# Gated cross attention: scores of two slots made in a row, and three results that share one PSUM bank

## The chip, the cores and the metric

The kernel runs on one core of a Trainium2 chip. Its time is the device time of one execution in microseconds (us), and the median of three executions is given. A core has a matrix engine (TensorE, PE in the profile, with its weight loads as a row of their own, PEld), a vector engine (VectorE, DVE), a scalar engine for activations (ScalarE, ACT), GpSimd (POOL) and SyncE (SP), which issues nearly all DMAs of this kernel. PE writes its results to PSUM, which has eight banks of 2 KB in each of 128 partitions; a bank holds 512 float32 columns. DVE and ACT read them from there.

## What is computed

Two layers of a gated block run over 8 sequences of 512 tokens with 256 features. The change lies in the first part, a cross attention with 16 heads of 64 features, whose weights are multiplied by a gate made from boxes:

```python
emb = box_relational_embedding(boxes)            # sines and cosines of log distances
g = relu(einsum('bnmd,hd->bhnm', emb, Wg) + bg)
q, k, v = projections of layernorm(x), ctx, ctx
a = einsum('bhqd,bhkd->bhqk', q, k) / sqrt(64)
mn = softmax(log(clip(g, 1e-6, None)) + a)       # = max(g, 1e-6) * exp(a), normalised
out = einsum('bhqk,bhkd->bqhd', mn, v) @ Wo.T + bo
x = x + tanh(g_xattn[0]) * out
```

After it come an attention with a mixture of experts, a second attention and a spiking feed-forward layer. The change leaves those alone.

## The kernel before

The cross attention is done in 32 steps `i`, one for each block of 128 queries. A step has 8 slots `p`, one for each pair of heads. Queries, keys and values have been projected ahead of the steps and lie in DRAM. The order of the instructions on PE, ACT and DVE is that of the program text (`tc.manual_schedule(engines=MANUAL)`, lines 547 to 595): each of these engines takes its instructions strictly in the order in which the loop writes them. The queue of SyncE is ordered by the compiler's planner. Buffers come from pools: a tile with a tag and `bufs=n` has n places, and a new tile of that tag waits until the last reader of the tile n before it is done. The pool `wk` (line 396) has two places unless a tile says otherwise, and the PSUM pool `ps` (line 397) has one.

What a slot p of step i does, in this order:

- `scores(i, p + 1)` (446): two matmuls over 64 rows each, one head each, into the two banks of `pS`; PE shows each as two records, so there are four. Then DVE takes the row maxima `nm` (459) and ACT makes the exponentials `e` (462) of both heads.
- `half()` (555), two or three times in a slot (`HALVES`): `gate_half` (422) makes a half block of the gates of the next step, two matmuls (four PE records) into one of two banks `pg`, and copies it to SBUF (441), on DVE in slots 0, 2 and 7 and on ACT in the others.
- `weigh(i, p)` (465), after the first half: eight transposes of `e` into the two banks of `pT`, then one DVE instruction of 1024 elements (473), which multiplies them by the gates into `at`.
- `values(i, p - 1)` (478), after the second half: eight matmuls (sixteen PE records) of the last slot's `at` with the values, into `po`. After an odd pair DVE takes the reciprocal `rec` of the sums (497) and makes the outputs `o` of four heads (499).
- `outputs` (504), at the end of slots 1, 3, 5, 7: two transposes of `o` into `pt`, and one ACT copy to `oT` (514).
- `mix` (516), at the end of slot 2: eight matmuls (sixteen records) of the last step's `oT` with `Wo` into `pw`, then on DVE the bias (526) and the residual sum (528), and a DMA to DRAM.
- `features`: pieces of the gate features of later steps. On DVE: `turns` (325) at the end of slot 0, `whole` and `rest` (328, 332) at the end of slot 1, `rest_sizes` (81) in slot 2 after the scores, `offsets` (310) at the end of slot 4 (three instructions) and slot 5 (two), `clip` (319) at the end of slot 6. On ACT: `sines` (338, 339) in slot 2, `sizes` (316) at the end of slot 5, `log` (322) in slot 7. Sines and logarithm need other activation tables than the exponentials, so a table load stands ahead of each and ahead of the next exponentials.

PSUM is full: `pS` 2 banks, `pT` 2, `po` 1, `pt` and `pw` 1 (tag "m"), `pg` 2.

Of the kernel before, what the change touches and what calls it, by code (L numbers as in the profile page):

```python
# [11 lines left out]
F32 = mybir.dt.float32  # L12
I32 = mybir.dt.int32
AF = mybir.ActivationFunctionType
ALU = mybir.AluOpType
# [4 lines left out]
P = 128  # L20
B, S, D = 8, 512, 256
NT = B * S // P
NQ = S // P
H, DK = 16, 64
# [50 lines left out]
PAIRS = H // 2  # L75
# [183 lines left out]
def gated_cross_attention(cx, a, tg, x1q, d, front):  # L259
# [3 lines left out]
    tc, nc, ident = cx.tc, cx.nc, cx.ident  # L263
    NSTEP = B * NQ
    NP = NB // 2
    with ExitStack() as es:
# [4 lines left out]
        wo = cp.tile([P, PAIRS, D], F32, name="wo")  # L271
# [80 lines left out]
        def features(j, *fns):  # L352
            for fn in fns:
                if 0 <= j < NSTEP:
                    fn(j)
# [40 lines left out]
        wk = es.enter_context(tc.tile_pool(name="xwk", bufs=2))  # L396
        ps = es.enter_context(tc.tile_pool(name="xps", bufs=1, space=PSUM))
        gates, qTs, xts, kTs, vTs = {}, {}, {}, {}, {}
        es_, ats, pos, oTs = {}, {}, {}, {}

        def load_key(i, p):
            i, p = i + p // PAIRS, p % PAIRS
            if i < NSTEP:
                kTs[i, p] = wk.tile([P, S], F32, name="kT", tag="kT", bufs=3)
                nc.sync.dma_start(out=kTs[i, p], in_=d["k"][i // NQ, p])

        def load_value(i, p):
            i, p = i + p // PAIRS, p % PAIRS
            if i < NSTEP:
                v = vTs[i, p] = wk.tile([P, NQ, 2, DK + 1], F32, name="v", tag="v", bufs=3)  # L410
                nc.sync.dma_start(out=v.rearrange("p k t d -> p (k t d)"), in_=d["v"][i // NQ, p])

        def load_queries(i):
            if i < NSTEP:
                qTs[i] = wk.tile([P, PAIRS, P], F32, name="qT", tag="qT")
                nc.sync.dma_start(out=qTs[i], in_=d["q"][i])
# [29 lines left out]
        def scores(i, p):  # L446

            i, p = i + p // PAIRS, p % PAIRS
            if i == NSTEP:
                return  # L450
            kT = kTs.pop((i, p))
            pS = ps.tile([P, 2, S], F32, name="pS", tag="s")
            for t in range(2):
                rows = slice(DK * t, DK * t + DK)
                nc.tensor.matmul(  # L455
                    pS[:, t, :], qTs[i][rows, p, :], kT[rows, :], start=True, stop=True
                )
            nm = wk.tile([P, 2], F32, name="nm", tag="nm")
            nc.vector.tensor_reduce(nm, pS, AX.X, ALU.max, negate=True)  # L459
            e = wk.tile([P, 2, S], F32, name="e", tag="e")  # L460
            for t in range(2):
                nc.scalar.activation(e[:, t, :], pS[:, t, :], AF.Exp, bias=nm[:, t : t + 1])  # L462
            es_[i, p] = e

        def weigh(i, p):

            e = es_.pop((i, p))
            pT = ps.tile([P, 2, NQ, P], F32, name="pT", tag="t")
            for t in range(2):
                for kc in range(NQ):  # L470
                    nc.tensor.transpose(pT[:, t, kc, :], e[:, t, kc * P : (kc + 1) * P], ident)  # L471
            at = wk.tile([P, 2, NQ, P], F32, name="at", tag="at")
            nc.vector.scalar_tensor_tensor(  # L473
                at, gates[i][:, 2 * p : 2 * p + 2], 1e-6, pT, ALU.max, ALU.mult
            )
            ats[i, p] = at

        def values(i, p):

            if p < 0:  # L480
                i, p = i - 1, p + PAIRS
            if i < 0:
                return
            at = ats.pop((i, p))
            v = vTs.pop((i, p))
            if p % 2 == 0:
                pos[i] = ps.tile([P, 4, DK + 1], F32, name="po", tag="o")
            po = pos[i]
            for t in range(2):
                for kc in range(NQ):  # L490
                    nc.tensor.matmul(  # L491
                        po[:, 2 * (p % 2) + t, :], at[:, t, kc, :], v[:, kc, t, :],
                        start=(kc == 0), stop=(kc == NQ - 1),
                    )
            if p % 2:
                rec = wk.tile([P, 4], F32, name="rec", tag="rec")
                nc.vector.reciprocal(rec, po[:, :, DK])
                o = wk.tile([P, 4, DK], F32, name="o", tag="o")
                nc.vector.tensor_tensor(  # L499
                    o, po[:, :, 0:DK], rec.unsqueeze(2).to_broadcast([P, 4, DK]), ALU.mult  # L500
                )
                oTs[i, p // 2] = o

        def outputs(i, g):

            if i < 0:
                return
            o = oTs.pop((i, g)).rearrange("p h d -> p (h d)")
            if g == 0:
                oTs[i] = wk.tile([P, PAIRS, P], F32, name="oT", tag="oT", bufs=1)  # L510
            pt = ps.tile([P, 2, P], F32, name="pt", tag="m")
            for c in range(2):
                nc.tensor.transpose(pt[:, c, :], o[:, c * P : (c + 1) * P], ident)
            nc.scalar.copy(oTs[i][:, 2 * g : 2 * g + 2, :], pt)  # L514

        def mix(i):
            if i < 0:
                return
            oT = oTs.pop(i)
            pw = ps.tile([P, D], F32, name="pw", tag="m")  # L520
            for c in range(PAIRS):
                nc.tensor.matmul(  # L522
                    pw, oT[:, c, :], wo[:, c, :], start=(c == 0), stop=(c == PAIRS - 1)
                )
            ot = wk.tile([P, D], F32, name="ot", tag="ot", bufs=1)
            nc.vector.tensor_tensor(ot, pw, bo, ALU.add)
            xo = wk.tile([P, D], F32, name="xo", tag="xo", bufs=1)
            nc.vector.scalar_tensor_tensor(xo, ot, tg[:, 0:1], xts.pop(i), ALU.mult, ALU.add)
            b, q = divmod(i, NQ)
            nc.sync.dma_start(out=x1q[q][b * P : (b + 1) * P, :], in_=xo)  # L530

# [1 line left out]
        HALVES = (3, 3, 3, 2, 2, 2, 2, 3)  # L535
        SINES, LOG = 2, 7

        for p in range(3):
            if p == 0:
                load_queries(0)  # L540
            load_key(0, p)
        for p in range(2):
            load_value(0, p)
        for k in range(2 * NB):
            gate_half(0, k, nc.vector.tensor_copy if k % 2 else nc.scalar.copy)
        scores(0, 0)
        with tc.manual_schedule(engines=MANUAL):
            for i in range(NSTEP):
                k = 0
                for p in range(PAIRS):  # L550
                    halves = list(range(k, k + HALVES[p]))
                    k += HALVES[p]
                    copy = nc.vector.tensor_copy if p in (SINES, LOG, 0) else nc.scalar.copy

                    def half():
                        if halves:
                            gate_half(i + 1, halves.pop(0), copy)

                    if p == 0:
                        load_queries(i + 1)  # L560
                        if (i + 3) % NQ == 0:
                            features(i + 3, lambda j: load_keys(j // NQ))
                    load_key(i, p + 3)
                    scores(i, p + 1)
                    if p == SINES:
                        features(i + 2, rest_sizes, sines)
                    if p == LOG:
                        features(i + 3, log)
                    half()
                    weigh(i, p)  # L570
                    half()
                    values(i, p - 1)
                    load_value(i, p + 2)
                    half()
                    if p in (3, 5, 7):
                        outputs(i, (p - 3) // 2)
                    if p == 1:
                        outputs(i - 1, 3)
                    if p == 0:
                        features(i + 2, turns)  # L580
                    if p == 1:
                        features(i + 2, whole, rest)
                    if p == SINES:
                        mix(i - 1)
                    if p == 3:
                        features(i + 2, load_products, place)
                        load_rest(i)
                    if p == 4:
                        features(i + 3, lambda j: offsets(j, 0, 3))
                    if p == 5:  # L590
                        features(i + 3, lambda j: offsets(j, 3, NP), sizes)
                    if p == 6:
                        features(i + 3, clip)
                    if i == NSTEP - 1:
                        front(p)
            values(NSTEP - 1, PAIRS - 1)
            outputs(NSTEP - 1, 3)
            mix(NSTEP - 1)


NG = 8
# [1250 lines left out]
```

## Time and profile before

| | |
|---|---|
| time, median of 3 executions | 2999.4 us (2994.04 to 2999.91) |
| profiled execution | 3000.78 us |
| span of its instructions | 2999.0 us |
| granted TensorE clock over the span | 0.984 |
| first and last gate matmul `pg` | 365.3 to 1929.1 us of the span |
| last matmul of `mix` | 1971.0 us |

The page of a profile gives the busy time of each engine, the chain of work that ended last (followed back from the last instruction, at each step to what released it), and groups of instructions by line, with count, busy time and mean duration. The trace behind it answers for any stretch: busy times in a window, the pieces of the chain in order of time, and a timeline of single engines, where `[0.76 <-issue]` after a row means that the engine had sat idle for 0.76 us, and what ended that. A matmul's row is longer than the time by which it holds up the next, because matmuls are pipelined: the distance between two starts is what counts.

### The profile page before, as it was taken

The page shows a single profiled execution, that of the slowest core. Times are in us where ns is not written, and L with a number is a line of the kernel's source. Part 1 is how long each engine was busy: PE and PEld are TensorE (multiplying, and loading weights), DVE is VectorE, ACT ScalarE, POOL GpSimd, SP SyncE. Part 2 cuts the span into 40 slices and gives each one's busy share as a digit, 9 for nine tenths or more (in the row PEclk, how much of TensorE's full clock was granted, in tenths as well). Part 3 has the DMA queues.
Part 4 walks back from the last instruction along what each step waited for, and adds up shares of the span by engine and source line. Part 5 has one row for each costly group of instructions (what it writes and reads, how often), then busy time and mean ns, then how long its engine had stood idle before and what let it go on. Part 6 is the DMA issues. An engine that isn't in the chain of part 4 may idle for free.

```text
span 2999.0 us, 39639 instructions
## 1 busy us (share of the span) xinstructions
PE 2913.7 (97%) x15398; PEld 2131.3 (71%) x15398; DVE 1831.4 (61%) x2863; ACT 1404.3 (47%) x2196; POOL 137.3 (5%) x137
## 2 busy tenths in 40 slices
PE   8999999999999999999999999989999998899998
PEld 3444578888888888888888888867766665456566
DVE  4422177777777777786877676557762011666758
ACT  4332256565656565656565655335431211243434
POOL 1000000000000000000000000000002110211100
PEclk9999999999999999999999999989989999899999
DMA  7766545555555464545464646361114432211100
GB/s 231 221 196 186 166 135 156 140 156 143 155 141 159 137 165 131 165 133 165 131 166 128 164 131 166 104 192 45 34 57 149 152 125 91 64 43 58 34 14 22
DMA packets 269068, 386.08 MB, mean 129 GB/s; under 512 B 55209, under 2 KB 132665, under 8 KB 266065
## 3 DMA queue, kind: packets, MB, share of 16 engines
q1 hardware_dynamic: 265808, 375.15, 43.3%
q0 software_dynamic: 3072, 8.39, 1.0%
q8 instruction: 122, 2.00, 0.3%
q14 instruction: 66, 0.53, 0.1%
HBM read 237.24 MB, written 78.07 MB: 105 GB/s over the span
## 4 chain that ended last, share of the span: by engine, by line
PE 80%; DVE 14%; DMA 2%; issue 2%; ACT 1%; SPq 1%; POOL 0%; DVEq 0%; ACTq 0%; POOLq 0%
PE pg L435 13%; PE po L491 11%; PE pk L212 7%; PE pS L455 7%; PE pT L471 5%; PE ph L1494 4%; PE ph L1273 4%; PE pw L522 4%; PE py L1282 4%; PE py L1509 4%; PE pv L227 4%; DVE nm L459 2%; PE pz L1466 2%; PE pq L686 2%; PE pS L1443 2%
## 5 line engine op out<-in xcount | busy, mean ns | idle before, releaser
L462 ACT ACTIVATE e<-pS,nm 128x512 f32<-128x512 f32 x512 | 324.2, 684 | 576.0 <-DVE nm L459 575.5
L435 PE MATMUL pg<-wst,emb 116*128 116x208 f32 (+1 forms) x2560 | 583.6, 351 | 6.7 <-DVE gate L441 5.6
L435 PEld LDWEIGHTS pg<-wst,emb 116*128 116x128 f32 x2560 | 416.2, 190 | 203.6 <-issue 81.5
L491 PEld LDWEIGHTS po<-v,at 128*128 128x128 f32 x4096 | 493.0, 192 | 0.1
L491 PE MATMUL po<-v,at 128*128 128x65 f32 x4096 | 485.6, 272 | 0.0
L459 DVE TENSOR_REDUCE nm<-pS 128x2 f32<-128x1024 f32 x256 | 312.7, 1221 | 178.0 <-PE pS L455 178.0
L473 DVE SCALAR_TENSOR_TENSOR at<-gate,pT 128x1024 f32<-128x1024 f32 x256 | 311.2, 1216 | 47.1 <-PE pT L471 46.1
L455 PE MATMUL pS<-kT,qT 64*128 64x512 f32 x1024 | 292.0, 642 | 5.1 <-ACT e L462 2.0
L471 PE MATMUL pT<-ident,e 128*128 128x128 f32 x2048 | 266.5, 273 | 0.0
L471 PEld LDWEIGHTS pT<-ident,e 128*128 128x128 f32 x2048 | 239.9, 141 | 14.0 <-DVE o L499 1.5
L441 DVE COPY gate<-pg 128x416 f32<-128x416 f32 (+1 forms) x289 | 164.8, 571 | 36.1 <-PE pg L435 32.5
L441 ACT COPY gate<-pg 128x416 f32<-128x416 f32 x351 | 166.7, 530 | 35.9 <-PE pg L435 33.3
L1286 DVE TENSOR_TENSOR ye<-py,b 128x256 f32<-128x256 f32 x32 | 13.6, 425 | 208.3 <-PE py L1282 208.3
L1277 ACT ACTIVATE hT<-ph,eb 128x512 f32<-128x512 f32 x64 | 44.0, 687 | 178.1 <-PE ph L1273 172.9
L212 PE MATMUL pk<-ctxT,wk__129 128*128 128x512 f32 x256 | 114.7, 603 | 8.5 <-DMA ctxT<-in_ctxT 7.2
L1494 PE MATMUL ph<-xnT,wf 128*128 128x512 f32 (+2 forms) x320 | 118.7, 513 | 1.7 <-ACT xnT L1364 1.5
L62 POOL TENSOR_TENSOR ln_rs<-ln_ve,mhalf 128x4 f32<-128x4 f32 x24 | 24.4, 1015 | 2068.5 <-DVE ln_ve L61 1987.2
L522 PE MATMUL pw<-wo,oT 128*128 128x256 f32 x512 | 115.9, 379 | 0.5 <-ACT oT L514 0.5
L1273 PE MATMUL ph<-dT,w 128*128 128x512 f32 x256 | 112.0, 595 | 2.9 <-DVE dT L1262 2.9
L212 PE MATMUL pk<-xnT,wq 128*128 128x512 f32 x256 | 113.0, 594 | 1.1 <-ACT st L216 0.9
L227 PE MATMUL pv<-wv,ctxT 128*128 128x512 f32 x256 | 114.0, 594 | 0.0
L455 PEld LDWEIGHTS pS<-kT,qT 64*128 64x128 f32 x1024 | 77.9, 184 | 50.5 <-issue 36.0
(251 smaller groups left out, 3996.7 us busy)
## 6 DMA issues: line engine op xcount, KB each, us to landing
v<-vdr SPq DMA_DIRECT2D x256, 260.0 KB
kT<-kdr SPq DMA_DIRECT2D x256, 256.0 KB
emb<-lt SPq DMA_DIRECT2D x64, 520.0 KB
emb<-nt SPq DMA_DIRECT2D x64, 520.0 KB
vdr<-vs SPq DMA_DIRECT2D x8, 2080.0 KB
kdr<-st SPq DMA_DIRECT2D x64, 256.0 KB
qdr<-st SPq DMA_DIRECT2D x64, 256.0 KB
qT<-qdr SPq DMA_DIRECT2D x32, 512.0 KB
```

What stands on the lines that cost most here:

```text
L212: nc.tensor.matmul(pk, w[:, c, m * P : (m + 1) * P], src[:, c, :], start=(c == 0), stop=(c == 1))
L227: nc.tensor.matmul(pv, ctxT[:, c, kc * P : (kc + 1) * P], wv[:, c, n * 512 : (n + 1) * 512], start=(c == 0), stop=(c == 1),)
L435: nc.tensor.matmul(pg[:, c, 0 : nq * H], embs[i % 2][R, blk // 2, blk % 2, kc * P : (kc + 1) * P], wst[i % 2][R, q0 * H : (q0 + nq) * H], ...
L441: copy(gates[i][:, :, 2 * hf : 2 * hf + 2, q0 : q0 + nq].rearrange("p h k q -> p k h q"), pg[:, :, 0 : nq * H].rearrange("p k (q h) -> p k ...
L455: nc.tensor.matmul(pS[:, t, :], qTs[i][rows, p, :], kT[rows, :], start=True, stop=True)
L459: nc.vector.tensor_reduce(nm, pS, AX.X, ALU.max, negate=True)
L462: nc.scalar.activation(e[:, t, :], pS[:, t, :], AF.Exp, bias=nm[:, t : t + 1])
L471: nc.tensor.transpose(pT[:, t, kc, :], e[:, t, kc * P : (kc + 1) * P], ident)
L473: nc.vector.scalar_tensor_tensor(at, gates[i][:, 2 * p : 2 * p + 2], 1e-6, pT, ALU.max, ALU.mult)
L491: nc.tensor.matmul(po[:, 2 * (p % 2) + t, :], at[:, t, kc, :], v[:, kc, t, :], start=(kc == 0), stop=(kc == NQ - 1),)
L522: nc.tensor.matmul(pw, oT[:, c, :], wo[:, c, :], start=(c == 0), stop=(c == PAIRS - 1))
L1494: nc.tensor.matmul(ph[:, 0:n], wf[:, c, f * P : (f + 1) * P], xnT[:, c, tok], start=(c == 0), stop=(c == 1),)
```

## The change

The scores of slots p + 2 and p + 3 are made together at the start of each even slot p, so `pS` gets two places (four banks). Maxima and exponentials become a function of their own, `exps`: those of p + 2 are made in slot p, in an even slot after the scores, in an odd slot after the first `weigh`. `weigh` works on one head at a time through a single bank `pT`, with a half block between the two heads. One bank, `bank`, is taken once and holds `po` (columns 0 to 259) and a field of 128 columns that `pt` and `pw` share. `outputs` and `mix` go through that field in two turns each, with a half block between them where there is one. The keys are loaded four slots ahead with four places. The tile `e` keeps the pool's two places.

```diff
+        bank = ps.tile([P, S], F32, name="po")
+        po = bank[:, 0 : 4 * (DK + 1)].rearrange("p (h d) -> p h d", d=DK + 1)
+        pt = pw = bank[:, 3 * P : 4 * P]
...
-                kTs[i, p] = wk.tile([P, S], F32, name="kT", tag="kT", bufs=3)
+                kTs[i, p] = wk.tile([P, S], F32, name="kT", tag="kT", bufs=4)
...
-            pS = ps.tile([P, 2, S], F32, name="pS", tag="s")
+            pS = pSs[i, p] = ps.tile([P, 2, S], F32, name="pS", tag="s", bufs=2)
             for t in range(2):
                 rows = slice(DK * t, DK * t + DK)
                 nc.tensor.matmul(
                     pS[:, t, :], qTs[i][rows, p, :], kT[rows, :], start=True, stop=True
                 )
+
+        def exps(i, p):
...
+            pS = pSs.pop((i, p))
             nm = wk.tile([P, 2], F32, name="nm", tag="nm")
             nc.vector.tensor_reduce(nm, pS, AX.X, ALU.max, negate=True)
             e = wk.tile([P, 2, S], F32, name="e", tag="e")
...
-        def weigh(i, p):
+        def weigh(i, p, t):
...
+            pT = ps.tile([P, NQ, P], F32, name="pT", tag="t")
+            for kc in range(NQ):
+                nc.tensor.transpose(pT[:, kc, :], e[:, t, kc * P : (kc + 1) * P], ident)
...
             nc.vector.scalar_tensor_tensor(
-                at, gates[i][:, 2 * p : 2 * p + 2], 1e-6, pT, ALU.max, ALU.mult
-            )
-            ats[i, p] = at
+                ats[i, p][:, t], gates[i][:, 2 * p + t], 1e-6, pT, ALU.max, ALU.mult
+            )
...
-        def outputs(i, g):
+        def outputs(i, g, c):
...
+            nc.tensor.transpose(pt, o[:, c * P : (c + 1) * P], ident)
+            nc.scalar.copy(oTs[i][:, 2 * g + c, :], pt)
+
+        def mix(i, n):
...
+            oT, cols = oTs[i], slice(n * P, (n + 1) * P)
             for c in range(PAIRS):
                 nc.tensor.matmul(
+                    pw, oT[:, c, :], wo[:, c, cols], start=(c == 0), stop=(c == PAIRS - 1)
+                )
...
+            nc.vector.tensor_tensor(xo[:, cols], pw, bo[:, cols], ALU.add)
+            if n == 1:
+                nc.vector.scalar_tensor_tensor(
+                    xo, xo, tg[:, 0:1], xts.pop(i), ALU.mult, ALU.add
+                )
...
-                    load_key(i, p + 3)
-                    scores(i, p + 1)
+                    load_key(i, p + 4)
+                    if p % 2 == 0:
+                        scores(i, p + 2)
+                        scores(i, p + 3)
+                        exps(i, p + 2)
                     if p == SINES:
                         features(i + 2, rest_sizes, sines)
+                    half()
+                    weigh(i, p, 0)
+                    if p % 2:
+                        exps(i, p + 2)
                     if p == LOG:
                         features(i + 3, log)
                     half()
-                    weigh(i, p)
-                    half()
+                    weigh(i, p, 1)
                     values(i, p - 1)
                     load_value(i, p + 2)
+                    g = {3: (i, 0), 5: (i, 1), 7: (i, 2), 1: (i - 1, 3)}.get(p)
+                    if g:
+                        outputs(*g, 0)
+                    if p == SINES:
+                        mix(i - 1, 0)
                     half()
-                    if p in (3, 5, 7):
-                        outputs(i, (p - 3) // 2)
-                    if p == 1:
-                        outputs(i - 1, 3)
+                    if g:
+                        outputs(*g, 1)
+                    if p == SINES:
+                        mix(i - 1, 1)
```

## The prediction

> **What bounds the kernel now.** I read the page first, then a window of one step, then the chain inside a step, then single rows. The page says that PE carries the chain:
>
> ```profile
> PE 2913.7 (97%) x15398; PEld 2131.3 (71%) x15398; DVE 1831.4 (61%) x2863; ACT 1404.3 (47%) x2196; POOL 137.3 (5%) x137
> PE 80%; DVE 14%; DMA 2%; issue 2%; ACT 1%; SPq 1%; POOL 0%; DVEq 0%; ACTq 0%; POOLq 0%
> ```
>
> A step of the cross attention takes 50.0 us (from one `mix` to the next), and in it PE has next to no free time, DVE a quarter:
>
> ```profile
> core 0: us, PE busy (x) PEld busy (x) DVE busy (x) ACT busy (x) POOL busy (x), PEclk, DMA share, GB/s
> 1440.90:1490.90 50.00, 49.83 (x333) 41.55 (x332) 37.64 (x46) 30.55 (x41) 0.00 (x0) 1.00 0.53 144
> ```
>
> The chain inside slot 5 is PE piece after piece, so whatever PE newly waits for is added in full:
>
> ```profile
> 1463.45 1.06 PE pS L455 x4
> 1464.51 0.90 PE pg L435 x4
> 1465.41 0.88 PE pT L471 x8
> 1466.29 0.70 PE pg L435 x4
> 1466.99 1.73 PE po L491 x16
> 1468.73 0.23 PE pt L513 x2
> ```
>
> **What two scores in a row save.** The scores' entry and exit show as gaps in PE's rows:
>
> ```profile
> 1424.03 0.30 PEld L491 LDWEIGHTS po<-v,at 128*128 128x128 f32 x2
> 1424.40 0.30 PEld L455 LDWEIGHTS pS<-kT,qT 64*128 64x128 f32 x4
> 1425.46 0.65 PEld L435 LDWEIGHTS pg<-wst,emb 116*128 116x128 f32 x4 [0.76 <-issue]
> ```
>
> The last values matmul starts at 1424.20, so its 65 columns have streamed by 1424.26; the score weights load only at 1424.40 (0.15 lost) and need 0.11. Two pairs of records then stream 0.43 each (the pitch of a 512-column record), to 1425.37; the gate weights load at 1425.46 (0.10 lost) and need 0.11 unhidden. A block costs 1.31, two in a row 2.17, against 2.62 less the 0.05 of an ordinary change of matmul: 0.40 saved. Four times a step that is 1.6 us, or 52 us over 32 steps. The split transposes, turns and `mix` have as many columns as before, and records of 128 columns follow at 0.11, so they cost PE nothing by themselves.
>
> **What the new order makes PE wait for.** Durations: L473 takes 1.22 us for 1024 elements; half of it lies near the nearest row of 512 elements from PSUM, 0.69:
>
> ```profile
> L473 DVE SCALAR_TENSOR_TENSOR at<-gate,pT 128x1024 f32<-128x1024 f32 x254 | 308.8, 1216 | 46.8 <-PE pT L471 45.8
> L729 DVE TENSOR_TENSOR sm<-pS,mask 128x512 f32<-128x512 f32 x30 | 20.7, 690 | 40.1 <-PE pS L724 40.1
> ```
>
> A turn's ACT copy (369 ns for 256 columns) I take at 0.25 for 128; bounds 0.18 and 0.37. A reader starts 0.21 after the last record has streamed; PE resumes 0.06 after a reader's end (DVE `gate` ends at 1448.19, PE loads at 1448.25) and pays its weight load of 0.11: together 0.38 around the work. On DVE and ACT the next instruction starts some 0.08 to 0.14 before the end of the last.
>
> *The bank of transposes.* `weigh` of head 1 may write only when DVE has read head 0: 0.38 + 0.69 = 1.07, covered by one half block, 0.70. PE waits 0.36 in every slot even if DVE is free at once. (Between nothing, if DVE began reading before the last transpose, which no row shows, and 0.36; I take 0.36.)
>
> *The exponentials.* `e` has two places, and `exps(p + 2)` needs that of `e(p)`, so ACT waits for the second `weigh` of slot p. Queued behind it are the ACT copies of the gate blocks, and the next slot's first block waits for a place in `pg`.
>
> *The shared field.* The second turn of `outputs` waits for ACT's copy of the first, with whatever stands ahead of that copy on ACT. In slot 7 that is the logarithm; before, nobody waited:
>
> ```profile
> 1429.07 1.28 ACT L322 ACT_TABLE_LOAD   x1
> 1430.36 2.34 ACT L322 ACTIVATE lt<-lt 116x2560 f32<-116x2560 f32 x1
> 1432.61 0.36 ACT L514 COPY oT<-pt 128x256 f32<-128x256 f32 x1
> ```
>
> *The shared bank.* Here a rule of the Trainium skill speaks against the change: "PSUM — Partial Sum Buffer", section "PSUM bank collisions raise a hardware error", wants engines kept apart by semaphores per bank and quadrant, not per address. The nearest row has `mix` in a bank of its own, running while DVE still reads `po`:
>
> ```profile
> 1449.06 1.46 PE L522 MATMUL pw<-wo,oT 128*128 128x256 f32 x6
> 1449.95 0.42 DVE L499 TENSOR_TENSOR o<-po,rec 128x256 f32<-128x256 f32 x1
> ```
>
> By address `mix` would go on at once: 0. By the rule it waits for `rec` and `o`: 0.21 + 0.62 + 0.17 = 1.0 in slot 2. I take the rule, because one tile is guarded as a whole bank; that is 32 us of the forecast.
>
> **One step as a timetable**, with time 0 at slot 4 after slot 3's last turn. PE blocks: half 0.70, `weigh` of a head 0.44, values 1.79, a turn 0.11, half of `mix` 1.74.
>
> Slot 4: scores to 1.96, half to 2.87, transposes to 3.31; DVE 3.52 to 4.21; PE resumes at 4.38 instead of 4.01: wait 0.37. `weigh` ends at 4.81, exponentials at 5.02, gate copies from 6.16 to 6.69 and 7.08. Values end at 6.60; `rec`, `o` and three offsets (0.46 each) keep DVE to 8.72.
>
> Slot 5: first half waits for the copy, 6.86: 0.26. Transposes end at 8.00, DVE is free at 8.72 and done at 9.41: PE waits 8.70 to 9.58, 0.88. `nm(7)` follows to 10.54, ACT's exponentials 10.60 to 11.74, a gate copy to 12.13, so the turn sent at 11.92 is copied by 12.38 and the second starts at 12.54: 0.62. End 12.65.
>
> Slot 6, like slot 4: 0.37; values end at 19.25, `clip` keeps DVE from 20.0 to 21.4.
>
> Slot 7: gate copy 0.26. DVE takes the gate copy at 21.4, the first head at 21.9 to 22.6; PE comes at 21.35 and resumes at 22.76: 1.41. `nm(9)` to 23.72, exponentials 23.78, table load 24.92, logarithm to 28.55; the first turn, sent at 25.1, is copied by 28.70; the second starts at 28.86 instead of 25.80: 3.06. End 28.97.
>
> Slot 0: 0.42. It ends at 36.33 with `turns` on DVE to 38.5. Slot 1: transposes end at 37.47, DVE takes them at 38.5 to 39.2, PE resumes at 39.36 instead of 38.17: 1.19. `nm(3)`, second head, `whole` and `rest` keep DVE to 44.95.
>
> Slot 2 starts at 42.5; `nm(4)` 44.95, `rest_sizes` to 47.48, gate copy to 47.98, first head to 48.67: PE resumes at 48.84 instead of 46.50, 2.33; then `mix` 1.0. Slot 3: 0.36 and for the turn (table load, exponentials and a gate copy before it) 0.62; end 61.53.
>
> Waits: 0.37 + 1.76 + 0.37 + 4.73 + 0.42 + 1.19 + 3.33 + 0.98 = 13.15. Against 1.6 saved: a step of 61.5, +11.5. DVE's own extra (0.15 for each split `at`) is in these times. Steps 29 to 31 lack features, and the last its gate blocks, so that nothing covers a round trip of transposes: +7, +4, +7. Sum: 29 × 11.5 + 18 = 352; 3000.8 + 352 = 3353 for the profiled execution (span 2999.0 and 1.8 around it). The median stands 1.4 lower: 3351, forecast 3350.
>
> The keys (four places) hide as before: k(p + 4) can be loaded once k(p) is scored, in an even slot p − 2 or before. In the trace one key waited 6.69 us from issue to landing, about a slot; a longer slot gives more room. I cost it at nothing; without that cover it is up to some 2 us a step.
>
> **The rivals.** *Faster:* readers keep up, waits stay under 0.2 a slot, and the 52 us show: 2949. For it: DVE is free a quarter and ACT 40% of a step. Against it: the order is fixed, and 1.07 does not fit behind 0.70. It would decide if each first head's round trip came down to the half block, and turns were copied at once. Chance 0.04; near no change (waits of just 1.6 a step) 0.02.
>
> *Only the bare round trips:* the backlogs of features find slack, and PE pays 0.36 in 256 slots (92 us) and 0.6 in 128 turns (77): 3000 + 169 − 52 = 3118. Against it: in slots 0 to 2 the chain before runs over DVE's features. Chance 0.12, with anything up to 3230.
>
> *Worse:* waits that the timetable doesn't hold, a key late in each step (2 × 32 = 64) or a cooler clock: the page "TensorE: Matmul & The Clock Gate", part 1, has the clock halve after an idle window of about 3.4 us, and slot 7's wait is 3.06; half clock for 1.7 us of a step is 54. Together 3468. The trace (granted clock 1.00 in these steps) can't show it. Chance 0.10 above 3430.
>
> The timetable itself 0.72, within 3230 to 3430 (waits off by 3 us a step). A difference of 0.2% is about what can be told from none here. Faster 0.04, same 0.02, slower 0.94.
>
> **What would show it.** Score records come eight in a row, and the gaps after them halve. L473's successor has 512 instances near 690 ns; PE waits for it at least 0.3 in nearly every slot, most in slots 7, 1 and 2. PE waits for ACT's `oT` about 3 us in slot 7. PE's share in a step falls to near 80%. I am wrong if a step is under 54 us, if the exponentials start before the second `weigh`, or if the second turn doesn't wait for the logarithm.

## The result, and the profile after

The changed kernel takes 3493.6 us (median of four, 3488.7 to 3495.9), against 2996.7 us for the kernel before (median of four, 2990.1 to 2999.9): the ratio is 1.166, with a 95% interval of 1.1645 to 1.1674. It is slower, as forecast, but by 497 us where 351 were forecast, and it lies above the range of 3230 to 3430 us.

The page of the changed kernel: PE has the same work and a smaller share, and the chain now runs over DVE and ACT for a third of the span.

```profile
PE 3049.0 (87%) x15910; PEld 2194.0 (63%) x15910; DVE 1868.6 (54%) x3151; ACT 1427.7 (41%) x2324; POOL 137.3 (4%) x137
...
PE 62%; DVE 23%; ACT 9%; issue 3%; DMA 1%; SPq 0%; POOL 0%; ACTq 0%; DVEq 0%; POOLq 0%
...
L473 ACT ACTIVATE e<-pS,nm 128x512 f32<-128x512 f32 x512 | 324.6, 684 | 791.0 <-PE pT L481 491.4
...
L486 DVE SCALAR_TENSOR_TENSOR at<-gate,pT 128x512 f32<-128x512 f32 x512 | 350.0, 684 | 140.2 <-PE pT L481 139.9
L481 PEld LDWEIGHTS pT<-ident,e 128*128 128x128 f32 x2048 | 238.2, 142 | 259.8 <-DVE at L486 248.6
...
L520 PEld LDWEIGHTS po<-ident,o 128*128 128x128 f32 x256 | 43.3, 169 | 196.5 <-ACT oT L521 195.5
...
L529 PEld LDWEIGHTS po<-wo,oT 128*128 128x128 f32 x1024 | 134.9, 210 | 31.6 <-DVE o L508 29.7
```

The columns of the groups are count, busy time, mean ns of one, then the idle time just before them and what ended most of it. The half-size `at` takes 684 ns (0.69 us had been taken). Three waits are new on PE's weight loads, and they are the three that were named: transposes for DVE's `at` (249 us), turns for ACT's `oT` (196), `mix` for DVE's `o` (30). The exponentials wait for PE's second `weigh`, as forecast.

One step, and in it the 3.4 us that follow slot 7 (engines' busy times in each window, then the granted clock, DMA share and GB/s):

```profile
core 0: us, PE busy (x) PEld busy (x) DVE busy (x) ACT busy (x) POOL busy (x), PEclk, DMA share, GB/s
1260.70:1327.30 66.60, 54.70 (x345) 44.17 (x345) 38.58 (x54) 32.59 (x45) 0.00 (x0) 0.93 0.41 112
1300.50:1303.90 3.40, 3.40 (x9) 1.11 (x9) 1.23 (x1) 0.40 (x2) 0.00 (x0) 0.61 0.15 14
```

PE waits 12 of 66.6 us, and the granted clock, 1.00 in a step before, is 0.93. From step 1 to step 28 a step takes 64.6 to 67.2 us with one exception of 70.2, 65.8 in the mean, where it took 49.85 before: 447 of the 488 us by which the two profiled executions differ. What stands ahead of the first `mix` adds 20 us and the last three steps 23; what follows takes 2 us less.

Slot 7 on PE shows what happens (start, duration, then the idle time before):

```profile
1296.50 0.76 PE L439 MATMUL pg<-wst,emb 116*128 116x176 f32 x4
1300.48 0.33 PE L520 MATMUL po<-ident,o 128*128 128x128 f32 x1 [3.22 <-ACT oT L521]
1300.74 1.61 PE L459 MATMUL pS<-kT,qT 64*128 64x512 f32 x4
```

and on ACT in the same stretch:

```profile
1296.64 1.28 ACT L322 ACT_TABLE_LOAD   x1
1297.94 2.34 ACT L322 ACTIVATE lt<-lt 116x2560 f32<-116x2560 f32 x1
1300.18 0.25 ACT L521 COPY oT<-po 128x128 f32<-128x128 f32 x1
```

The copy of the first turn stands behind the logarithm, and PE waits 3.22 us for it; forecast were 3.06. Then come the scores of slot 0, and there pairs of records start 0.84 us apart instead of 0.43: half clock. Slot 2 of the same step has the longest wait for DVE, and the wait of `mix`:

```profile
1322.07 1.11 PE L481 MATMUL pT<-ident,e 128*128 128x128 f32 x4 [2.25 <-DVE at L486]
1322.98 3.51 PE L500 MATMUL po<-v,at 128*128 128x65 f32 x16
1327.29 1.01 PE L529 MATMUL po<-wo,oT 128*128 128x128 f32 x3 [0.80 <-DVE o L508]
```

The values take 3.51 us here and 1.90 in slot 7: from 1322.0 to 1326.3 us the granted clock was 0.50.

Against the timetable, slot by slot, the starts of weight loads in this step give the waits of slots 4 to 7 within 0.2 us of the forecast: the second head of slot 5 at 1281.0 (forecast 1281.1, with the timetable's time 0 at 1271.6), the second turn of slot 5 at 1284.1 (1284.0), the second head of slot 7 at 1294.2 (1294.3), its second turn at 1300.5 (1300.4). From there the trace runs late: 1.5 us by the end of slot 0, 3.7 by the start of `mix`. One more miss is in slot 3, where the second turn was to wait 0.6 and waits 1.85:

```profile
1268.31 1.28 ACT L473 ACT_TABLE_LOAD   x1 [1.83 <-DVE nm L470]
...
1271.15 0.28 ACT L521 COPY oT<-po 128x128 f32<-128x128 f32 x1
...
1271.49 0.33 PE L520 MATMUL po<-ident,o 128*128 128x128 f32 x1 [1.85 <-ACT oT L521]
```

The table load of the exponentials waits for the maxima itself. The timetable had put it in ACT's idle time before them, and in the kernel before that is where it stands; in slot 3 it starts while DVE has yet to begin with them:

```profile
1403.34 1.28 ACT L462 ACT_TABLE_LOAD   x1
1403.61 1.22 DVE L459 TENSOR_REDUCE nm<-pS 128x2 f32<-128x1024 f32 x1 [0.19 <-PE pS L455]
1404.87 1.27 ACT L462 ACTIVATE e<-pS,nm 128x512 f32<-128x512 f32 x2 [0.24 <-DVE nm L459]
```

So the change itself moved the load behind the wait.

The theory to be tested: the waits are those of the timetable, plus 1.3 us a step for the table load, plus what the clock loses when PE idles. The rivals are that the clock is a symptom without a price, and that the split into smaller instructions, or sharing a bank as such, makes the loss.

### The profile page after: what moved, and what is told of

The parts are those of the page before. It is cut to its first block, busy times and chain, and to the rows that moved or that the text cites. A ratio compares the mean times of both kernels' runs of the same rounds, so it can differ in the third digit from the quotient of the medians.

```text
span 3486.9 us, 41294 instructions
## 1 busy us (share of the span) xinstructions
PE 3049.0 (87%) x15910; PEld 2194.0 (63%) x15910; DVE 1868.6 (54%) x3151; ACT 1427.7 (41%) x2324; POOL 137.3 (4%) x137
## 4 chain that ended last, share of the span: by engine, by line
PE 62%; DVE 23%; ACT 9%; issue 3%; DMA 1%; SPq 0%; POOL 0%; ACTq 0%; DVEq 0%; POOLq 0%
PE po L500 7%; PE pS L459 7%; PE pk L212 6%; DVE at L486 5%; PE pg L439 5%; DVE nm L470 5%; PE pT L481 4%; PE po L529 4%; PE ph L1519 3%; PE ph L1298 3%; PE py L1307 3%; PE py L1534 3%; PE pv L227 3%; ACT e L473 3%; ACT lt L322 2%
## 5 line engine op out<-in xcount | busy, mean ns | idle before, releaser
L439 PEld LDWEIGHTS pg<-wst,emb 116*128 116x128 f32 x2560 | 427.2, 194 | 133.3 <-issue 52.7
L500 PE MATMUL po<-v,at 128*128 128x65 f32 x4096 | 500.5, 277 | 0.4 <-ACT oT L521 0.4
L481 PE MATMUL pT<-ident,e 128*128 128x128 f32 x2048 | 326.3, 282 | 169.1 <-DVE at L486 157.7
L486 DVE SCALAR_TENSOR_TENSOR at<-gate,pT 128x512 f32<-128x512 f32 x512 | 350.0, 684 | 140.2 <-PE pT L481 139.9
L459 PE MATMUL pS<-kT,qT 64*128 64x512 f32 x1024 | 303.4, 711 | 0.0
L520 PE MATMUL po<-ident,o 128*128 128x128 f32 x256 | 78.7, 307 | 169.9 <-ACT oT L521 169.1
L520 PEld LDWEIGHTS po<-ident,o 128*128 128x128 f32 x256 | 43.3, 169 | 196.5 <-ACT oT L521 195.5
L529 PE MATMUL po<-wo,oT 128*128 128x128 f32 x1024 | 142.3, 297 | 26.2 <-DVE o L508 25.0
L459 PEld LDWEIGHTS pS<-kT,qT 64*128 64x128 f32 x1024 | 99.5, 207 | 90.3 <-issue 74.4
L529 PEld LDWEIGHTS po<-wo,oT 128*128 128x128 f32 x1024 | 134.9, 210 | 31.6 <-DVE o L508 29.7
```

The source lines that it names most:

```text
L439: nc.tensor.matmul(pg[:, c, 0 : nq * H], embs[i % 2][R, blk // 2, blk % 2, kc * P : (kc + 1) * P], wst[i % 2][R, q0 * H : (q0 + nq) * H], ...
L459: nc.tensor.matmul(pS[:, t, :], qTs[i][rows, p, :], kT[rows, :], start=True, stop=True)
L481: nc.tensor.transpose(pT[:, kc, :], e[:, t, kc * P : (kc + 1) * P], ident)
L486: nc.vector.scalar_tensor_tensor(ats[i, p][:, t], gates[i][:, 2 * p + t], 1e-6, pT, ALU.max, ALU.mult)
L500: nc.tensor.matmul(po[:, 2 * (p % 2) + t, :], at[:, t, kc, :], v[:, kc, t, :], start=(kc == 0), stop=(kc == NQ - 1),)
L520: nc.tensor.transpose(pt, o[:, c * P : (c + 1) * P], ident)
```

## The experiments

**The parts alone, put into the kernel before.** First `weigh` by heads through one bank, with a half block between:

```diff
-            pT = ps.tile([P, 2, NQ, P], F32, name="pT", tag="t")
+            pT = ps.tile([P, NQ, P], F32, name="pT", tag="t", bufs=1)
...
-                    weigh(i, p)
+                    weigh(i, p, 0)
+                    half()
+                    weigh(i, p, 1)
```

> The kernel before with one part of the change alone: weigh by heads through a single bank with a half block between (one PSUM bank stays unused; scores, outputs and mix as before). Theory (PE waits for DVE's reading of the first head, and DVE is late by its features in slots 5, 7, 1, 2): the waits of the timetable, 0.37 + 0.88 + 0.37 + 1.41 + 0.42 + 1.19 + 2.33 + 0.36 = 7.3 us a step, with 1.7 more if the clock falls for a window after slot 2: 3210 at full clock, 3260 with it. Rival (PE pays only the bare round trip, 0.36 in 256 slots): 3090.

Measured: 3334.1 us, ratio 1.1127 (1.1089 to 1.1165). A step takes 60.2 us, 10.4 more than before; PE's waits for `at` show on its weight loads:

```profile
PEld pT L470 <- DVE at L475: 206.3, 186, 3.2
```

(total us between 500 and 1900 us, times, longest). The bare round trip is refuted, and the 7.3 us a step with a window of half clock fall short by 74 us: the waits of a step sum to 8.9 us, with 3.2 instead of 2.3 in slot 2, and half clock lasts 5.6 us a step instead of 3.4.

The same with two places for that bank-sized tile, `bufs=2`:

> As the last, but the single-bank tile of transposes has two places (the two banks of before). Theory (the wait for the place makes the loss, not the split): 2997 to 3015, the 0.15 us that DVE has more in each slot showing in slots 1 and 2 at most. Rival (two half-size instructions on DVE cost by themselves): 3040 or more.

Measured: 2994.3 us beside 2995.3, ratio 0.9996 (0.9986 to 1.0006): no difference. The split costs nothing that shows; the single place costs all of it.

Then `outputs`, `mix` and `po` in one bank, in turns, with the functions of the changed kernel:

```diff
+        bank = ps.tile([P, S], F32, name="po")
+        po = bank[:, 0 : 4 * (DK + 1)].rearrange("p (h d) -> p h d", d=DK + 1)
+        pt = pw = bank[:, 3 * P : 4 * P]
```

> The kernel before with another part alone: outputs, turns and mix in one bank, in two turns and two halves (one PSUM bank unused; scores and weigh as before). Theory: the second turn waits for ACT's copy behind the logarithm in slot 7 (2.9), 0.6 and 0.75 in slots 3 and 5, and mix waits for DVE's rec and o in slot 2 (2.4): 6.7 us a step, +200: 3195 at full clock; with one or two windows of half clock a step (1.7 each) 3250 to 3300. Rival (mix goes on at once since it writes other columns, and the turns are copied in time except in slot 7): 3090.

Measured: 3306.2 us, ratio 1.1034 (1.0997 to 1.107).

```profile
PE po L512 <- ACT oT L513: 82.7, 69, 2.8
PE po L521 <- DVE o L500: 55.1, 23, 2.4
```

(The last column is again the longest.) In one step the turns wait 2.8 us in slot 7, 0.8 in slot 3, 0.5 in slot 5, and `mix` 2.4 for DVE's reading of other columns of its bank: 6.5, where 6.7 were expected. Half clock lasts 8.9 us a step in the mean. So in this program `mix` does wait for a reader of the bank and not only of its own columns; no run leaves that wait out, so whether the chip needs it is not shown.

The two parts together, 339 + 311, are more than the whole change. It is not that one wait covers another: PE is idle 6.4 us in a step of the first part, 6.0 in one of the second and 11.9 in the step of the changed kernel shown above. But half clock lasts 5.6 and 8.9 us a step in the parts and 6.3 in the whole, and the parts lack the saving of the scores.

**The clock.** In the changed kernel PE repeats the matmuls of a gate half block in the two longest waits:

```diff
-            for c in range(2):
+            for c in list(range(2)) * times:
...
-                    half()
+                    half(4 if p == SINES else 1)
                     weigh(i, p, 1)
...
-                    half()
+                    half(5 if p == LOG else 1)
```

> The changed kernel, but PE repeats the matmuls of one gate half block in the places where it waits longest: five times in all for the third half block of slot 7, four times for the second of slot 2 (same operands, same result, written again). It adds 2.8 + 2.1 us of PE work a step and takes no wait away. Theory (the idle stretches halve the clock, which costs about half of the 189 us at half clock): the granted clock in the attention returns to near 1.00, and the time falls by 60 to 90 us, to 3405 to 3435, although PE has more to do. Rival (the waits alone cost the time, the clock is a symptom without a price): 3490 or a few us more.

Measured: 3454.0 us, ratio to before 1.153 (1.1497 to 1.1564). That is 40 us faster than the changed kernel with 4.9 us more PE work a step. Two of its steps:

```profile
1180.10:1244.60 64.50, 57.15 (x372) 46.86 (x372) 38.61 (x54) 30.95 (x44) 0.00 (x0) 0.97 0.42 116
1309.20:1372.10 62.90, 55.55 (x372) 46.11 (x372) 38.62 (x54) 30.99 (x44) 0.00 (x0) 1.00 0.45 118
```

They do the same work. The first holds one window of 3.4 us at half clock, the second none, and the difference is 1.6 to 1.7 us: that is the price of a window. The changed kernel's steps with one window take 64.6 us too, so the repeated matmuls fit into the waits. The gain was below the 60 to 90 expected because the fall moved: with the waits of slots 7 and 2 filled, 24 of the 28 steps had a window after the unfilled wait of slot 3, where the changed kernel has 52 windows in these steps.

**The logarithm** moved behind the second turn:

```diff
-                    if p == LOG:
-                        features(i + 3, log)
...
                         outputs(*g, 1)
+                    if p == LOG:
+                        features(i + 3, log)
```

> The changed kernel, with the logarithm of slot 7 moved behind the second turn of outputs on ACT. Theory (PE waits for ACT's copy behind the logarithm, and the idle stretch then halves the clock for one window of 3.4 us): the 3.5 us gap before the second turn in slot 7 goes to under 0.5 and the slow scores of slot 0 (0.84 us a pair of records instead of 0.43) go too: about 3.2 + 1.6 = 4.8 us a step, 29 steps, -140 us: 3355. Rival (the slow scores have nothing to do with the wait): only 3.2 x 29 = -93: 3400.

Measured: 3415.8 us, ratio to before 1.1403 (1.137 to 1.1436), 78 us faster than the changed kernel, less than either expected. The gap of slot 7 is gone and so are slot 0's slow scores. But now 30 of the 32 steps have half clock in slot 2 (in values and `mix`), where 8 had it, and every second one has it after slot 3's wait as well: half clock lasts 8.5 us a step instead of 6.3. A step takes 63.1 us.

**The table load** brought forward by an exponential of one column after the sines and after the logarithm:

```diff
                         features(i + 2, rest_sizes, sines)
+                        nc.scalar.activation(warm, warm, AF.Exp, scale=0.0)
...
                         features(i + 3, log)
+                        nc.scalar.activation(warm, warm, AF.Exp, scale=0.0)
```

> The changed kernel, with an exponential of one column after the sines and after the logarithm on ACT, so that the table load of the exponentials is done before the maxima arrive. Theory (in slot 3 the load stands behind the wait for nm and delays ACT's copy of the first turn): the second turn's gap in slot 3 falls from 2.1 to about 0.9 us, -1.3 x 30 = -38 us: 3455. Rival (the load is hidden anyway, another wait takes its place): 3490.

Measured: 3458.2 us, ratio 1.1544 (1.1511 to 1.1578). The number fits, but not for the expected reason alone: slot 3's gap fell from 2.1 to 0.85, slot 7's grew from 3.5 to 5.0, since the load there now stood ahead of the copy, and slot 2 lost its half-clock windows. By itself this run shows no price of the load.

So filling and load were tried together, with the early load after the sines only, which is the run that decides:

> The changed kernel with PE's repeated gate matmuls in slots 7 and 2 (as in the run with filled waits) and an exponential of one column after the sines alone, so that the table load of slot 3 stands ahead of the wait for nm. Theory (the timetable of the prediction is right at full clock but for that load): the second turn's gap in slot 3 falls from 2.1 to 0.9 us, no half-clock window follows it any more, and every step takes 61.5 to 61.7 us instead of 64.6: 3370 to 3380. Rival (half clock comes from something else than idle stretches): steps of 63.3, 3415.

Measured: 3380.9 us, ratio 1.1297 (1.1275 to 1.132). Nearly every step takes 61.7 us, at full clock:

```profile
1149.00:1210.60 61.60, 55.52 (x372) 46.08 (x372) 38.62 (x54) 31.05 (x45) 0.00 (x0) 1.00 0.46 121
```

That is the step of the prediction's timetable (61.5), and 113 us less than the changed kernel. In steps 1 to 28 four windows of half clock are left of 52. Against the full-clock step of the run with filled waits alone (62.9) the load is worth 1.3 us.

**Three places for `e`** (and three for the keys, to make room):

```diff
-            e = wk.tile([P, 2, S], F32, name="e", tag="e")
+            e = wk.tile([P, 2, S], F32, name="e", tag="e", bufs=3)
```

> The changed kernel with three places for e (and three for the keys, to make room in SBUF), so that ACT's exponentials need not wait for the second weigh of the slot. Theory: the first half blocks of slots 5 and 7 no longer wait for a gate copy behind them, 0.26 each: -0.5 x 30 = -15: 3478, and whatever a shift of the half-clock windows adds or takes (30 either way). Rival (the wait for e is what makes the step long): 3430 or less.

Measured: 3492.3 us, ratio 1.1655 (1.1611 to 1.1698): no different from the changed kernel. ACT's wait of 491 us for `weigh` is gone and the time is the same. The 0.26 us twice a step may have been saved and spent again: windows of half clock rose from 52 to 57.

**Scores one slot at a time** in the changed kernel, `scores(i, p + 2)` at the start of every slot:

> The changed kernel without the scores in a row: scores(p + 2) at the start of every slot, the rest as changed. Theory (two in a row save 0.40 us a pair, and PE is on the path): between +25 us (where DVE or ACT set the end of a slot) and +52 us: 3518 to 3545. Rival (pairing saves nothing): 3490; a lower time would say that pairing itself costs.

Measured: 3606.0 us, ratio 1.2038 (1.2003 to 1.2073), 112 us slower, far more than expected. It is no measure of the saving: half clock grew from 6.3 to 17.3 us a step, and the wait for DVE in slot 2 to 3.1 us. In the next pair the single scores are the faster ones.

**Another order**, with all that the change does to PSUM: values between the two heads of `weigh`, exponentials at the start of each slot, the logarithm after the turn, the halves of `mix` moved to the end of slot 2 and into slot 3. It also has three places for `e` and for the keys, and the gate copies of slot 2 are on ACT, those of slot 4 on DVE.

```diff
+                    exps(i, p + 2)
+                    half()
+                    if p == 3:
+                        mix(i - 1, 1)
                     weigh(i, p, 0)
...
                     values(i, p - 1)
...
                     weigh(i, p, 1)
+                    half()
```

> All that the change does with PSUM and with the scores in a row, but another order: values between the two heads of weigh (1.8 us or more behind which DVE reads the first head), exponentials at the start of every slot (three places for e, three for keys), rest_sizes after the first head of slot 2 and the sines after its last gate block, logarithm after the second turn, the halves of mix at the end of slot 2 and after the first half block of slot 3; gate copies of slot 2 on ACT, those of slot 4 on DVE. Theory (only the waits behind single places make the loss): PE 48.3 us a step and 2 to 3 us of waits left in slots 1 to 3, 50.5 to 51.5 at full clock: 3020 to 3050. Rival (sharing banks and fields costs whatever the order): 3150 or more.

Measured: 3141.7 us, ratio 1.0496 (1.0478 to 1.0513). Then the same with scores one slot at a time:

> As the last, with scores one slot at a time. Theory (two in a row save 0.40 us of PE a pair): 20 to 50 us more than the last, 3050 to 3090. Rival (no saving, or hidden behind the waits that are left): the same as the last within 10 us.

Measured: 3096.3 us, ratio 1.0345 (1.0325 to 1.0364). The order, with the moved gate copies, takes back 352 of the 497 us (three places for `e` alone took back nothing), so sharing does not cost that much whatever the order; the 145 us that are left are more than the 23 to 53 expected. With scores in a row it is 45 us slower than without. At full clock its steps take 53.4 us and the other's 52.4: in such steps the paired order waits 2.0 us for a turn in slot 3 and 1.0 for a head in slot 5, the single one 0.8 and nothing in the same places. Why was not tested.

**The saving by itself** needed a kernel in which nothing waits. With the gate blocks left out (the gates of the first block of queries serve for all, so the result is another) two banks are free, and everything but the scores can stay in the banks of before. The base:

> The kernel before with work left out in the steps: no gate half blocks (the gates of the first block of queries serve for all) and no gate features, so that two PSUM banks are free; everything else as before, scores one slot at a time. It is the base for the next run. PE should have 36 us of work a step and wait for nothing: 2550 to 2600.

and the pair, whose exponentials stay in the slots of before:

```diff
-                    scores(i, p + 1)
...
+                    if p % 2:
+                        scores(i, p + 1)
+                        scores(i, p + 2)
+                    exps(i, p + 1)
```

> The same work left out, and the scores of two slots in a row into four banks (keys loaded four ahead with four places), with transposes, outputs, turns and mix in the banks of before. Theory (two in a row save the drains and weight loads of one entry, 0.40 us a pair, four a step): 1.6 us a step less than the base, -51 us in 32 steps. Rival (no saving: drains and loads are paid for each block of scores): the same as the base within 8 us.

Measured: 2530.2 us for the base, 20 below what was expected, and 2486.3 for the pair, with ratios to the kernel before of 0.8452 (0.8438 to 0.8466) and 0.8302 (0.8288 to 0.8315). In the base, then in the pair, PE is busy throughout from 800 to 1200 us:

```profile
800.00:1200.00 400.00, 400.00 (x2838) 312.75 (x2837) 252.69 (x297) 133.37 (x230) 0.00 (x0) 1.00 0.50 144
```

```profile
800.00:1200.00 400.00, 400.00 (x2963) 331.23 (x2963) 268.85 (x311) 138.86 (x240) 0.00 (x0) 1.00 0.51 151
```

In 400 us the pair gets 4% more records through. Its step is 33.5 us against 35.0: 1.43 less, or 0.36 for two scores in a row, four times a step.

## Why the prediction was right in direction and wrong in size

- *What bounds the kernel, and that new waits of PE add in full:* right.
- *Two scores in a row save 0.40 us, 52 us in all:* right in mechanism; 0.36 and 44 us where PE waits for nothing. In the changed kernel the saving is buried.
- *The bank of transposes, the shared field, the shared bank:* right. The bank of transposes was shown by its part alone, the field and the shared bank together by theirs, and the run with two places shows that the single place, not the split, is paid for. For `mix` the forecast by bank held against the one by address: 1.0 us of wait was forecast, and its weight load waits 0.99 in the step above.
- *The exponentials wait for `weigh`:* right, but at 0.26 us twice a step it was already small, and three places gained nothing measurable.
- *The keys at nothing:* right. PE's scores wait for no key in the changed kernel.
- *The table load in slot 3 in ACT's idle time:* wrong, the smaller of two failed steps. It was read from the kernel before, where it holds. In the changed kernel the load starts only when the maxima are there, and costs 1.3 us a step, about 36 us in steps 1 to 28.
- *A cooler clock, set apart as a rival with chance 0.10:* this is the step that failed most. The sum was made at full clock throughout, although it put 13 us of waits into a step. Half clock costs 65.8 − 62.9 = 2.9 us a step in the mean, 82 us in those 28 steps. Counted the other way, the trace has 52 windows in them, which at 1.6 to 1.7 us each are 83 to 88 us. The rival named the place, slot 7, and priced one window at 1.7, which was right; it did not reckon with slots 2 and 3, and it belonged into the likeliest case. That its total, 3468, came near is luck: 64 us of it were for a late key, which did not come.

The sum, for steps 1 to 28: 322 forecast + 36 + 82 = 440 of the 447 measured. (The 82 are what is left above the full-clock step, so what the sum tests is that step, 61.5 + 1.3 against 62.9.) What the forecast missed outside these steps was not followed up. The rival with only the bare round trips is refuted by its part alone (3334 where it has 3090). No version that does the whole work beat the kernel before: the one with heads split over two places equals it, and the freed banks that would let the scores pay are not there as long as the gates need theirs. Whether an order exists in which the shared banks cost less than the 44 us was not settled.

## What to carry to other kernels

Count, for each buffer that a change leaves with one place, the whole round trip (last write, the reader's queue, the read, the restart) against the work that stands between two uses, and look up what else stands in the reader's queue: here a logarithm and feature arithmetic of several us. A wait on the path has a second price if it makes the matrix engine idle: put the clock into the likeliest case as soon as a timetable holds waits like those of 2 us here. And an experiment that shortens one wait can move the clock's windows elsewhere, so compare steps at equal clock, or fill the waits.

## What the hardware showed unexpectedly

The clock fell in windows of 3.41 us, on a fixed beat: in the changed kernel's attention the 39 falls began whole multiples of 3.413 us apart (those in slot 0, for one, at 447.93, 512.78, 577.63 and 645.90 us, which is 19, 19 and 20 times), and half clock lasted one to four such windows. One such window cost 1.6 to 1.7 us. A stretch idle from end to end was not needed: taking gaps between starts of PE records over 0.55 us (less 0.25) as idle, the windows before a fall held 1.2 to 3.2 us of idle in the changed kernel; windows with up to 2.0 us of it passed without a fall, so these runs give no threshold. In the run with filled waits, a single gap of 2.1 us in slot 3 brought a fall in most steps. The Trainium skill's page "TensorE: Matmul & The Clock Gate" (part 1) speaks of an idle window of about 3.4 us; here windows that were idle for about half of it were enough. Before the change there was one such window of half clock in the attention's 1590 us.

An activation table load can run ahead of what its activation waits for, or behind it. In the kernel before, the loads of slot 3 began 1.5 us before the maxima were there, and in the run with heads in one bank those after the sines began 5.9 to 7.6 us before. In the changed kernel the loads waited for the maxima, 1.8 us in slot 3 and 2.4 to 3.1 in slot 0. In these traces a semaphore instruction of the exponentials' line stands in ACT's queue ahead of each load that waited, and none ahead of those that ran early (each run's very first load aside); the line has 61 such instructions in the kernel before and 256 in the changed one. Why the program has them there was not tested.
